# The last expert of a mixture-of-experts layer: scatters made independent, its side work in a new order, part of the output summed by transfers

## Chip, core and metric

The kernel runs on one core of one Trainium2 chip. The metric is the device time of one execution in microseconds (us). A core has five engines that run their own instruction streams: TensorE (PE, matrix products), VectorE (DVE), ScalarE (ACT), GpSimd (POOL) and SyncE (SP, which only issues transfers here). They meet through semaphores. Transfers (DMAs) are issued by SP or by POOL; the indirect ones, with a list of row numbers, come from POOL.

## What is computed

Four layers follow each other, each normalized and added to a running `x` of 4096 tokens by 256 numbers (float32). The change lies in the last one, an expert layer:

```python
    def _L1_ffn_ref(x, Wg, W1, b1, W2, b2):
        ...
        S = jax.nn.sigmoid(xt @ Wg).T
        G, I = jax.lax.top_k(S, k)                 
        ex = xt[I]
        hid = jax.nn.gelu(jnp.einsum('ekh,ehf->ekf', ex, W1) + b1[:, None, :], approximate=False)
        out = (jnp.einsum('ekf,efh->ekh', hid, W2) + b2[:, None, :]) * G[..., None]
        new_x = jnp.zeros_like(xt).at[I.reshape(-1)].add(out.reshape(-1, h))
        return new_x.reshape(b, l, h)
    ...
    x = x + _layernorm(_L1_ffn_ref(_layernorm(x, axis=-1), L1_ffn_Wg, L1_ffn_W1, L1_ffn_b1, L1_ffn_W2, L1_ffn_b2), axis=-1)
```

Each of 8 experts takes its own 1024 best tokens of the 4096. A token may be taken by several experts or by none; its expert outputs are summed, that sum is normalized over its 256 numbers, and `x` is added.

## The kernel before

Tokens lie in 8 blocks of 512 (`TB`), each block as 128 partitions by `NJ` = 4 rows; the blocks of `x` stay on chip as `xs[t]`. At the end of the attention stage `token_rows` (line 1163 and on) writes each block to DRAM twice: normalized rows to `tok_d` and `x` itself to `x_d`. Both are issued by SP.

The expert stage makes, for each expert, a list of its 1024 tokens (`List`), fetches their normalized rows by `List.fetch` (line 1497, eight indirect DMAs of 128 rows from POOL, into `got`), and works in two units of 512 tokens: `feed_forward(u)` with `u` from 0 to 15, expert `e = u // 2`, half `q = u % 2`. A unit has

- eight steps "f" (line 1669): products `ph` of 128 hidden features by 512 tokens, three PSUM buffers, each emptied by ACT with a Gelu into `hid` (line 1676);
- four steps "i" (line 1692): products `py` of 128 tokens by 256 numbers, two PSUM buffers, each emptied by DVE. PE also turns the rows of the next unit (line 1651) after two of them.

For experts 0 to 6, DVE adds the bias and multiplies by the gate into `y` (lines 1706, 1707), and POOL adds `y` to rows of a DRAM tensor `acc_d` by an indirect, accumulating DMA (line 1708). The framework sees each such scatter as a write to the whole of `acc_d`, so each one waits until the one before has landed.

Expert 7 does not scatter its sums. When its turn comes, `with_last_acc` reads `acc_d` back, block by block into `y = ys[t]` (`read_back`, line 1535, on SP; six buffers, of which four lie in the weights of expert 6), and also gathers the rows of expert 7's own tokens: into `accg` from `acc_d`, and into `xg` from `x_d`. Then all 4096 tokens are finished as though there were no expert 7:

- `all_stats(t)`: means and variances on DVE (lines 1526 to 1542), a power and a product on POOL (1530, 1543);
- `all_scaled(t, half)`: four normalizations per block on ACT (1549), in place;
- `all_out(t)`: DVE adds the block to `xs[t]` (1554), SP stores it to the output (1555), and the next block is read back into the freed buffer.

Meanwhile expert 7's tokens are finished on their own: `chosen_known` adds the gated bias to `accg` (1562), the product is added when it leaves PSUM (1718), and `chosen_out` normalizes, adds `xg` and overwrites the tokens' output rows by an indirect DMA (1574 to 1579), which must come after all stores of blocks.

In this stage PE, DVE and ACT run in the order in which the program lists them; POOL and SP are ordered by the framework's scheduler. `asides` is a table of what is listed after each step of expert 7's two units; `aside(u, kind, i)` runs it. In the table before, statistics of block t, its scalings and its sum are spread over steps (0, "f", 6) to (1, "f", 3); the biases of chunks 0 to 3 follow at (0, "f", 7) and (0, "i", 0), and the first four chunks leave at (1, "f", 5).

Of the kernel before, what the change touches and what calls it, by code (L numbers as in the profile page):

```python
# [9 lines left out]
F32 = mybir.dt.float32  # L10
# [8 lines left out]
P = 128  # L19
# [26 lines left out]
CAP = 2  # L46
NSEG = P // NE
NROUND = 15


def bucket_runs():
# [19 lines left out]
def kernel(  # L71
# [961 lines left out]
    with ExitStack() as st3:  # L1033
# [84 lines left out]
        def close(t, h, oT):  # L1118
# [43 lines left out]
                return scale_of("g", xs[t][:, i, :])  # L1162

            def token_rows(i, mean, rs):
                if i == 0:
                    gating["h"] = wk.tile([P, NJ, D], F32, tag="hg", name="hg")
                hg = gating["h"][:, i, :]
                nc.vector.tensor_scalar(hg, xs[t][:, i, :], mean, rs, ALU.subtract, ALU.mult)
                nc.sync.dma_start(tok_d[t * TB + i * P : t * TB + (i + 1) * P, 0:D], hg)
                if i == NJ - 1:  # L1170
                    nc.sync.dma_start(x_d[t * TB : (t + 1) * TB, :].rearrange("(j p) d -> p j d", p=P), xs[t])
                if i % 2:
                    beside.append(lambda: turn_gating(i - 1))
                if i == NJ - 1:
                    beside.append(gate)
# [133 lines left out]
    with ExitStack() as st4:  # L1309
# [132 lines left out]
        class List:  # L1442
# [53 lines left out]

            def fetch(self, dst, rows, c):

                nc.gpsimd.indirect_dma_start(  # L1499
                    out=dst,  # L1500
                    out_offset=None,
                    in_=rows[:, :],
                    in_offset=self.at_chunk(c),
                    bounds_check=NT - 1,
                    oob_is_err=True,
                )
# [2 lines left out]

        out_rows = out.flatten_outer_dims()
        accg = keep.tile([P, NC, D], F32, name="accg")
        xg = keep.tile([P, NC, D], F32, name="xg")
        few = st4.enter_context(tc.tile_pool(name="last", bufs=4))
        stores, ys, room_back = [], {}, []

        def stats_of(tag, tiles):

# [12 lines left out]

        def read_back(t):
            y = room_back[t % len(room_back)]
            nc.sync.dma_start(y, acc_d[t * TB : (t + 1) * TB, :].rearrange("(j p) d -> p j d", p=P))
            ys[t] = [y]

        def all_stats(t):
            y = ys[t][0]
            mv, rs = stats_of("c", [y[:, i, :] for i in range(NJ)])  # L1540
            ms = few.tile([P, NJ], F32, tag="msc", name="msc")
            nc.vector.tensor_scalar(ms, mv[:, :, 0], -1.0, None, ALU.mult)
            nc.gpsimd.tensor_tensor(ms, ms, rs, ALU.mult)
            ys[t] += [rs, ms]

        def all_scaled(t, half):
            y, rs, ms = ys[t]
            for i in (2 * half, 2 * half + 1):
                nc.scalar.activation(  # L1549
                    y[:, i, :], y[:, i, :], AF.Identity, bias=ms[:, i : i + 1], scale=rs[:, i : i + 1]  # L1550
                )

        def all_out(t):
            nc.vector.tensor_tensor(xs[t], xs[t], ys[t][0], ALU.add)  # L1554
            stores.append(nc.sync.dma_start(out_flat[t], xs[t]))
            if t + len(room_back) < NB:
                read_back(t + len(room_back))

        def chosen_known(ks):

            for k in ks:
                nc.vector.scalar_tensor_tensor(
                    accg[:, k, :],
                    mb2[:, NE - 1, :],
                    lists[NE - 1].got[k][:, D + NE - 1 : D + NE],
                    accg[:, k, :],
                    ALU.mult,
                    ALU.add,
                )

        def chosen_out(ks):
            mv, rs = stats_of("d", [accg[:, k, :] for k in ks])
            for i, k in enumerate(ks):
                nc.vector.tensor_scalar(accg[:, k, :], accg[:, k, :], mv[:, i, 0:1], None, ALU.subtract)
            for i, k in enumerate(ks):
                nc.vector.scalar_tensor_tensor(
                    xg[:, k, :], accg[:, k, :], rs[:, i : i + 1], xg[:, k, :], ALU.mult, ALU.add
                )
                scatter = nc.gpsimd.indirect_dma_start(
                    out=out_rows,  # L1580
                    out_offset=lists[NE - 1].at_chunk(k),
                    in_=xg[:, k, :],
                    in_offset=None,
                    bounds_check=NT - 1,
                    oob_is_err=True,
                )
                for store in stores:
                    tc.add_manual_dep(scatter.ins, store.ins.name, over, reason="in the place of")
                for other in replaced:
                    tc.declare_no_dep(scatter.ins, other.ins, reason="an expert's tokens are distinct")  # L1590
                replaced.append(scatter)

        over = mybir.DependencyInfo(mybir.DependencyClass.Sync, mybir.DependencyReason.DATA)
        replaced = []

        def with_last_rows():
            for c in range(NC):
                lists[NE - 1].fetch(xg[:, c, :], x_d, c)

        def with_last_acc():  # L1600

            for tag in ("w1", "w2"):
                free = we.tile([P, 2, NJ, D], F32, tag=tag, name=f"back_{tag}")
                room_back.extend(free[:, k] for k in range(2))
            room_back.extend(wk.tile([P, NJ, D], F32, tag="back", name="back") for _ in range(2))
            for t in range(len(room_back)):
                read_back(t)
            for c in range(NC):
                lists[NE - 1].fetch(accg[:, c, :], acc_d, c)

        def asides():
            at = {}

            def put(where, *steps):
                at.setdefault(where, []).extend(steps)

            places = [(0, "f", 6), (0, "f", 7), *((0, "i", i) for i in range(NJ)), (1, "f", 0), (1, "f", 1)]
            later = [(0, "f", 7), *((0, "i", i) for i in range(NJ)), (1, "f", 0), (1, "f", 1), (1, "f", 2)]  # L1620
            latest = [*((0, "i", i) for i in range(NJ)), (1, "f", 0), (1, "f", 1), (1, "f", 2), (1, "f", 3)]
            for t in range(NB):
                put(later[t], lambda t=t: all_scaled(t, 0))
                put(latest[t], lambda t=t: all_scaled(t, 1), lambda t=t: all_out(t))
                put(places[t], lambda t=t: all_stats(t))
            put((0, "f", 7), lambda: chosen_known((0, 1)))
            put((0, "i", 0), lambda: chosen_known((2, 3)))
            put((1, "f", 4), lambda: chosen_known((4, 5)))
            put((1, "f", 5), lambda: chosen_known((6, 7)), lambda: chosen_out((0, 1, 2, 3)))
            return at  # L1630

        beside_last = asides()

        def aside(u, kind, i):
            e, q = divmod(u, QPE)
            if e == NE - 1:
                for step in beside_last.get((q, kind, i), ()):
                    step()

        QPE = NC // NJ  # L1640
        xT = {}
# [13 lines left out]
        def feed_forward(u):  # L1655
# [32 lines left out]
            for i in range(NJ):  # L1688
# [12 lines left out]
                if i in (1, 2) and u + 1 < NE * QPE:  # L1701
                    turn(u + 1, i - 1)
                gates = lists[e].got[k][:, D + e : D + e + 1]
                if e < NE - 1:
                    y = wk.tile([P, D], F32, tag="y", name="y", bufs=4)
                    nc.vector.tensor_tensor(y, py, mb2[:, e, :], ALU.add)  # L1706
                    nc.vector.tensor_scalar(y, y, gates, None, ALU.mult)
                    nc.gpsimd.indirect_dma_start(  # L1708
                        out=acc_d[:, :],
                        out_offset=lists[e].at_chunk(k),  # L1710
                        in_=y,
                        in_offset=None,
                        bounds_check=NT - 1,
                        oob_is_err=True,
                        compute_op=ALU.add,
                    )
                else:
                    nc.vector.scalar_tensor_tensor(accg[:, k, :], py, gates, accg[:, k, :], ALU.mult, ALU.add)  # L1718
                    aside(u, "i", i)
                    if q:  # L1720
                        chosen_out((k,))

        lists[0].chunks()
        for part in range(4):
# [1 line left out]
            lists[0].collect(part)  # L1726
        lists[0].gather()
        for u in range(NE * QPE):
            if u == (NE - 1) * QPE:
                with_last_acc()  # L1730
            feed_forward(u)
            e, q = divmod(u, QPE)
            if u == (NE - 1) * QPE - 2:
                with_last_rows()
            if q == QPE - 1 and e + 2 < NE:
                weights.append(load_expert(e + 2))

# [33 lines left out]
```

## Time and profile before

| what | us |
|---|---|
| median of 3 runs (1650.67 to 1650.97) | 1650.72 |
| the profiled execution, own time | 1650.91 |
| its span, first to last instruction | 1648.8 |
| PE busy | 1550.9 (94%) |
| DVE busy | 926.6 (56%) |
| ACT busy | 634.3 (38%) |
| POOL busy | 399.7 (24%) |
| expert 7 begins on PE (unit 14) | 1565.45 |
| last product of expert 7 ends | 1639.64 |

A profile's line of a timeline has: start, length, engine, line of the kernel, operation, output<-inputs, shape, how many were merged, and in brackets how long that engine sat idle before it and what released it. "PEld" are weight loads, which run beside the products. Idle time of an engine counts only where another one then waits for it. The DMA share is the mean busy share of the core's 16 DMA engines.

### The profile page before, as it was taken

The page shows a single profiled execution, that of the slowest core. Times are in us where ns is not written, and L with a number is a line of the kernel's source. Part 1 is how long each engine was busy: PE and PEld are TensorE (multiplying, and loading weights), DVE is VectorE, ACT ScalarE, POOL GpSimd, SP SyncE. Part 2 cuts the span into 40 slices and gives each one's busy share as a digit, 9 for nine tenths or more (in the row PEclk, how much of TensorE's full clock was granted, in tenths as well). Part 3 has the DMA queues.
Part 4 walks back from the last instruction along what each step waited for, and adds up shares of the span by engine and source line. Part 5 has one row for each costly group of instructions (what it writes and reads, how often), then busy time and mean ns, then how long its engine had stood idle before and what let it go on. Part 6 is the DMA issues. An engine that isn't in the chain of part 4 may idle for free. (4 is left out here: it accounts for less than half of the span.)

```text
span 1648.8 us, 22341 instructions
## 1 busy us (share of the span) xinstructions
PE 1550.9 (94%) x8663; PEld 770.9 (47%) x8663; DVE 926.6 (56%) x2090; ACT 634.3 (38%) x1101; POOL 399.7 (24%) x434
## 2 busy tenths in 40 slices
PE   7999999999999999999999999922999999999986
PEld 3666666665222232323232222211766675766754
DVE  4555566663667787878787888776222122121245
ACT  3344444434554545454545454520211212112133
POOL 4123232322201020202011111012333332332643
PEclk9999999999999999999999999965999999999998
DMA  8300000000000000000000000050134233323362
GB/s 211 111 1 1 1 1 1 1 1 1 1 1 1 14 14 14 14 14 14 1 26 1 27 14 14 20 162 24 39 78 90 65 66 79 68 65 74 68 179 87
DMA packets 71028, 68.51 MB, mean 42 GB/s; under 512 B 23277, under 2 KB 65162, under 8 KB 70794
## 3 DMA queue, kind: packets, MB, share of 16 engines
q1 hardware_dynamic: 57760, 47.01, 9.4%
q0 software_dynamic: 12288, 19.15, 6.3%
q8 instruction: 68, 1.11, 0.3%
q10 hardware_dynamic: 874, 0.93, 0.2%
q14 instruction: 38, 0.31, 0.1%
HBM read 41.74 MB, written 25.33 MB: 41 GB/s over the span
## 5 line engine op out<-in xcount | busy, mean ns | idle before, releaser
L1233 DVE TENSOR_SCALAR w<-sc 128x1024 f32<-128x1024 f32 x256 | 312.7, 1222 | 97.4 <-PE sc L1223 65.1
L1232 ACT ACTIVATE w<-sc 128x512 f32<-128x512 f32 x512 | 278.0, 594 | 229.6 <-PE sc L1223 102.5
L1223 PE MATMUL sc<-qT,kT 32*128 32x512 f32 x2048 | 293.6, 639 | 1.4 <-ACT w L1232 0.8
L1239 PE MATMUL po<-w,vaug 128*17 128x512 f32 x2048 | 274.7, 598 | 1.3 <-DVE turned L1271 0.3
L1692 PE MATMUL py<-w,hid 128*128 128x256 f32 x1024 | 232.9, 384 | 6.9 <-DVE accg L1718 6.9
L1669 PE MATMUL ph<-xT,w 128*128 128x512 f32 (+1 forms) x544 | 228.5, 578 | 4.7 <-ACT hid L1676 4.2
L1676 ACT ACTIVATE hid<-ph,mb 128x512 f32<-128x512 f32 (+1 forms) x136 | 89.9, 661 | 345.6 <-PE ph L1669 342.7
L1692 PEld LDWEIGHTS py<-w,hid 128*128 128x128 f32 x1024 | 192.9, 192 | 40.2 <-DVE accg L1718 7.4
L1223 PEld LDWEIGHTS sc<-qT,kT 32*128 32x128 f32 x2048 | 80.8, 183 | 184.8 <-issue 170.7
L1669 PEld LDWEIGHTS ph<-xT,w 128*128 128x128 f32 x544 | 105.4, 195 | 118.8 <-issue 107.4
L1239 PEld LDWEIGHTS po<-w,vaug 128*17 128x17 f32 x2048 | 35.3, 95 | 200.3 <-issue 171.0
L1708 POOL DMA_INDIRECT acc_d<-y,idx x56 | 88.5, 1580 | 166.5 <-issue 139.5
L1706 DVE TENSOR_TENSOR y<-py,mb 128x256 f32<-128x256 f32 x56 | 23.4, 418 | 142.8 <-PE py L1692 135.5
L1499 POOL DMA_INDIRECT got<-tok_d,idx x64 | 65.8, 1028 | 151.6 <-DVE idx L1489 134.5
L1653 DVE COPY xT<-tp 128x512 f32<-128x512 f32 (+1 forms) x34 | 22.3, 660 | 90.9 <-PE tp L1651 90.9
L1059 POOL TENSOR_TENSOR rsg<-veg,mhalf 128x1 f32<-128x1 f32 x32 | 17.7, 553 | 219.5 <-DVE veg L1058 219.5
L683 PE MATMUL pg<-nT,wh 128*128 128x512 f32 x128 | 61.5, 613 | 1.5 <-ACT nT L622 1.5
L791 PE MATMUL py<-wo,oT 128*128 128x256 f32 x256 | 61.9, 385 | 0.0
L699 PE MATMUL pv<-wh,nT 128*128 128x512 f32 x128 | 59.7, 592 | 0.0
L1489 DVE CAST idx<-parts 128x8 int32<-128x8 f32 x8 | 1.3, 167 | 101.8 <-PE parts L1487 101.8
L791 PEld LDWEIGHTS py<-wo,oT 128*128 128x128 f32 x256 | 47.3, 190 | 17.2 <-issue 9.4
L564 POOL TENSOR_TENSOR x<-x,y 128x1024 f32<-128x1024 f32 x14 | 32.9, 2351 | 73.3 <-ACT y L553 73.3
(273 smaller groups left out, 1889.2 us busy)
## 6 DMA issues: line engine op xcount, KB each, us to landing
w<-in_L_ffn_W_dram SPq DMA_DIRECT2D x16, 1024.0 KB, 5.7
x<-in_L_attn_x_dram SPq DMA_DIRECT2D x8, 512.0 KB, 7.6
acc_d<-logits SPq DMA_DIRECT2D x8, 512.0 KB, 4.6
x_d<-x SPq DMA_DIRECT2D x8, 512.0 KB, 3.0
tok_d<-hg SPq DMA_DIRECT2D x32, 128.0 KB, 1.7
out_dram<-x SPq DMA_DIRECT2D x8, 512.0 KB, 2.9
back_w<-acc_d SPq DMA_DIRECT2D x6, 512.0 KB, 5.4
wh<-in_L_attn_Wh_dram SPq DMA_DIRECT2D x2, 512.0 KB
```

The source lines that it names most:

```text
L683: nc.tensor.matmul(pg, lhsT=wh[:, c, HID + e * P : HID + (e + 1) * P], rhs=d["nT"][:, c, :], start=(c == 0), stop=(c == DC - 1),)
L699: nc.tensor.matmul(pv, lhsT=d["nT"][:, c, i * P : (i + 1) * P], rhs=wh[:, c, 0:HID], start=(c == 0), stop=(c == DC - 1),)
L791: nc.tensor.matmul(py, lhsT=d["oT"][:, e, :], rhs=wo[:, e, :], start=(e == 0), stop=(e == EC - 1))
L1223: nc.tensor.matmul(sc, lhsT=row["kT"][t][rows, r, kt * P : (kt + 1) * P], rhs=row["qT"][rows, t, qh * TB : (qh + 1) * TB], start=True, sto ...
L1232: nc.scalar.activation(w[:, j, :], sc, AF.Relu)
L1233: nc.vector.tensor_scalar(w[:, 2:4, :], pair, 0.0, None, ALU.max)
L1239: nc.tensor.matmul(po[32 * j : 32 * j + HD + 1, :], lhsT=row["v"][:, kt, HQ * t + 2 * j + r, :], rhs=w[:, j, :], start=(kt == 0), stop=(kt ...
L1499: nc.gpsimd.indirect_dma_start(out=dst, out_offset=None, in_=rows[:, :], in_offset=self.at_chunk(c), bounds_check=NT - 1, oob_is_err=True,)
L1669: nc.tensor.matmul(ph, lhsT=w1[:, c, f * P : (f + 1) * P], rhs=xT[u][:, c, h * n : (h + 1) * n], start=(c == 0), stop=(c == DC - 1),)
L1676: nc.scalar.activation(hid[:, f, h * n : (h + 1) * n], ph, AF.Gelu, bias=mb1[:, e * FC + f : e * FC + f + 1])
L1692: nc.tensor.matmul(py, lhsT=hid[:, f, i * P : (i + 1) * P], rhs=w2[:, f, :], start=(f == 0), stop=(f == FC - 1),)
L1708: nc.gpsimd.indirect_dma_start(out=acc_d[:, :], out_offset=lists[e].at_chunk(k), in_=y, in_offset=None, bounds_check=NT - 1, oob_is_err=Tr ...
```

## The change

Four things are changed.

1. In `token_rows`, the first `ADDED` = 5 blocks of `x` are also stored to the output tensor, in four pieces each, during the attention stage.
2. For those blocks `all_out` does not add on DVE: POOL issues a DMA that adds the normalized block to the output rows in DRAM. The read-back of these blocks puts four neighbouring tokens into one partition, so that its rows and those of the accumulating store are 4 KB long. Blocks 5 to 7 go as before.
3. The eight scatters of expert 6 are declared independent of each other, the first still waiting for expert 5's last. What reads `acc_d` afterwards (the read-backs and the gathers into `accg`) is made to wait for all eight. `xg` is now fetched between expert 6's two units, and `accg` in three parts, four, two and two chunks.
4. The table of side work is written out anew, and POOL too runs in listed order from expert 6 on.

```diff
+ADDED = 5
...
             def token_rows(i, mean, rs):
+                if t < ADDED:
+                    nc.sync.dma_start(out_flat[t][:, i, :], xs[t][:, i, :])
...
+        out_tokens = out.flatten_outer_dims()
+        out_rows = out_tokens.rearrange("(t p j) d -> t p j d", p=P, j=NJ)
...
+        def after_all(one, others):
+            for other in others:
+                tc.add_manual_dep(one.ins, other.ins.name, all_rows, reason="all rows")
+
+        def beside_each_other(one, others):
+            for other in others:
+                tc.declare_no_dep(one.ins, other.ins, reason="an expert's tokens are distinct")
+            others.append(one)
...
-            nc.sync.dma_start(y, acc_d[t * TB : (t + 1) * TB, :].rearrange("(j p) d -> p j d", p=P))
+            rows = "(p j) d -> p j d" if t < ADDED else "(j p) d -> p j d"
+            after_all(nc.sync.dma_start(y, acc_d[t * TB : (t + 1) * TB, :].rearrange(rows, p=P)), summed)
...
         def all_out(t):
-            nc.vector.tensor_tensor(xs[t], xs[t], ys[t][0], ALU.add)
-            stores.append(nc.sync.dma_start(out_flat[t], xs[t]))
+            y = ys[t][0]
+            if t < ADDED:
+                stores.append(nc.gpsimd.dma_start(out_rows[t], y, accum_op=ALU.add))
+            else:
+                nc.vector.tensor_tensor(xs[t], xs[t], y, ALU.add)
+                stores.append(nc.sync.dma_start(out_flat[t], xs[t]))
             if t + len(room_back) < NB:
                 read_back(t + len(room_back))
...
+        def fetch_acc(*cs):
+            for c in cs:
+                after_all(last.fetch(accg[:, c, :], acc_d, c), summed)
...
+        def chosen_out(*ks):
+            for k in ks:
                 scatter = nc.gpsimd.indirect_dma_start(
-                    out=out_rows,
-                    out_offset=lists[NE - 1].at_chunk(k),
+                    out=out_tokens,
+                    out_offset=last.at_chunk(k),
...
+                after_all(scatter, stores)
+                beside_each_other(scatter, replaced)
...
+        front, back = (0, 1), (2, 3)
+        beside_last = {
+            (0, "f", 5): [(all_stats, 0)],
+            (0, "f", 6): [(all_stats, 1)],
+            (0, "f", 7): [(all_scaled, 0), (known, 0), (all_stats, 2), (fetch_acc, 4, 5)],
+            (0, "i", 0): [(all_out, 0), (all_scaled, 1), (known, 1), (all_stats, 3)],
+            (0, "i", 1): [(all_out, 1), (all_scaled, 2), (known, 2), (all_stats, 4), (fetch_acc, 6, 7)],
+            (0, "i", 2): [(all_out, 2), (all_scaled, 3), (known, 3)],
+            (0, "i", 3): [(all_out, 3), (all_scaled, 4), (all_stats, 5)],
+            (1, "f", 0): [(all_out, 4)],
+            (1, "f", 1): [(all_scaled, 5, front), (all_stats, 6)],
+            (1, "f", 2): [(all_scaled, 5, back), (all_stats, 7)],
+            (1, "f", 3): [(all_scaled, 6, front), (all_out, 5)],
+            (1, "f", 4): [(all_scaled, 6, back), (chosen_stats, 0, 1, 2, 3)],
+            (1, "f", 5): [(all_scaled, 7, front), (all_out, 6)],
+            (1, "f", 6): [(all_scaled, 7, back), (chosen_less_mean, 0, 1, 2, 3)],
+            (1, "f", 7): [(all_out, 7), (known, 4, 5, 6, 7)],
+            (1, "i", 0): [(chosen_sum, 0, 1, 2, 3), (chosen_stats, 4), (chosen_less_mean, 4), (chosen_out, 0, 1, 2, 3)],
+            (1, "i", 1): [(chosen_sum, 4), (chosen_stats, 5), (chosen_less_mean, 5), (chosen_out, 4)],
+            (1, "i", 2): [
+                (chosen_sum, 5), (chosen_out, 5), (chosen_stats, 6), (chosen_less_mean, 6), (chosen_sum, 6), (chosen_out, 6)
+            ],
+            (1, "i", 3): [(chosen_stats, 7), (chosen_less_mean, 7), (chosen_sum, 7), (chosen_out, 7)],
+        }
...
+                if e == NE - 1:
                     nc.vector.scalar_tensor_tensor(accg[:, k, :], py, gates, accg[:, k, :], ALU.mult, ALU.add)
                     aside(u, "i", i)
-                    if q:
-                        chosen_out((k,))
+                    continue
...
+                if e == NE - 2:
+
+                    beside_each_other(scatter, summed)
...
         for u in range(NE * QPE):
-            if u == (NE - 1) * QPE:
-                with_last_acc()
+            e, q = divmod(u, QPE)
+            if u == (NE - 2) * QPE:
+                st4.enter_context(tc.manual_schedule(engines={engines.Pool}))
+            elif u == (NE - 1) * QPE - 1:
+                for c in range(NC):
+                    last.fetch(xg[:, c, :], x_d, c)
+            elif u == (NE - 1) * QPE:
+                begin_last()
             feed_forward(u)
-            e, q = divmod(u, QPE)
-            if u == (NE - 1) * QPE - 2:
-                with_last_rows()
```

The arithmetic of the old helper functions is kept: `known` is `chosen_known`, and `chosen_stats`, `chosen_less_mean`, `chosen_sum` and the new `chosen_out` are the four parts of the old `chosen_out`. `begin_last` is `with_last_acc` with only the first four gathers into `accg`.

## The prediction

> **What bounds the kernel now.** I read the page first (busy slices), then stretches of the last expert, then the timelines of TensorE (PE), VectorE (DVE) and GpSimd (POOL) there, then the DMA view. Times are us from the span's start. Page, busy tenths:
>
> ```profile
> PE   7999999999999999999999999922999999999986
> PEclk9999999999999999999999999965999999999998
> ```
>
> PE is full except in the routing stage (slices 27, 28), which the change does not touch, and at the end. Only the end is at stake. The stretches below are a whole unit of 512 tokens of expert 6; then the last expert: first products of its unit 14, second products of 14, first of 15, second of 15, the tail. Columns: sum, PE, PEld, DVE, ACT, POOL busy, PE clock, DMA share, GB/s.
>
> ```profile
> 1537.02:1565.45 28.43, 28.43 (x106) 19.02 (x104) 4.31 (x10) 5.50 (x8) 16.32 (x14) 1.00 0.37 65
> 1565.45:1579.18 13.73, 13.73 (x33) 6.08 (x32) 0.85 (x2) 4.81 (x7) 4.74 (x4) 1.00 0.25 30
> 1579.18:1603.92 24.74, 17.79 (x73) 14.81 (x72) 16.00 (x56) 7.77 (x15) 14.01 (x16) 0.86 0.79 256
> 1603.92:1625.65 21.73, 17.55 (x33) 6.94 (x32) 16.13 (x58) 13.31 (x26) 6.84 (x9) 0.84 0.42 144
> 1625.65:1639.64 13.99, 13.98 (x65) 11.97 (x63) 8.65 (x26) 0.69 (x1) 9.39 (x11) 1.00 0.16 57
> 1639.64:1648.80 9.16, 0.00 (x0) 0.00 (x0) 1.99 (x6) 0.00 (x0) 2.09 (x3) 0.74 0.08 30
> ```
>
> An undisturbed unit is 28.43, its first half 13.73, so the second half is 14.70. Third row: 24.74 - 14.70 = 10.0 lost. Fourth: 21.73 - 13.73 = 8.0 lost. So PE loses 18.0, and a tail of 9.2 follows. Where, in PE's timeline:
>
> ```profile
> 1588.44 3.72 PE L1692 MATMUL py<-w,hid 128*128 128x256 f32 x16 [1.76 <-DVE accg L1718]
> ...
> 1597.79 6.29 PE L1692 MATMUL py<-w,hid 128*128 128x256 f32 x16 [5.19 <-DVE accg L1718]
> ...
> 1617.35 8.46 PE L1669 MATMUL ph<-xT,w 128*128 128x512 f32 x12 [3.63 <-ACT hid L1676]
> ```
>
> PE waits for DVE to free one of two `py` buffers, then for ACT to free a `ph`. DVE and POOL say why:
>
> ```profile
> 1566.11 0.42 DVE L1707 TENSOR_SCALAR y<-y,got 128x256 f32<-128x256 f32 x1
> 1582.18 1.41 DVE L1526 BATCH_NORM_STATS2 stc<-back_w 128x6 f32<-128x256 f32 x4 [15.65 <-DMA back_w<-acc_d]
> ...
> 1587.51 0.48 DVE L1562 SCALAR_TENSOR_TENSOR accg<-mb,got,accg 128x256 f32<-128x256 f32 x1 [1.12 <-DMA accg<-acc_d,idx]
> ```
>
> ```profile
> 1569.95 1.55 POOL L1708 DMA_INDIRECT acc_d<-y,idx  x1 [3.02 <-issue]
> 1574.44 1.56 POOL L1708 DMA_INDIRECT acc_d<-y,idx  x1 [2.94 <-issue]
> 1579.03 1.08 POOL L1499 DMA_INDIRECT accg<-acc_d,idx  x1 [3.03 <-DMA acc_d<-y,idx]
> ...
> 1642.55 1.05 POOL L1579 DMA_INDIRECT out_dram<-xg,idx  x1 [0.81 <-DVE xg L1576]
> ```
>
> The last `y` of expert 6 is ready at 1566.5, but its scatter starts at 1574.44, because each waits for the landing of the one before (pitch 4.6 against 1.56 of issue). It lands at 1578.24 (3.8 after its start); only then are the sums read back, and DVE has idled 15.65. Late, DVE has statistics and five whole-block adds between PE's evictions. What a scatter-add costs the DMA engines, 1556 to 1578:
>
> ```profile
> q0 software_dynamic: 720, 0.66, 26.5%
> ```
>
> That is 26.5% x 22 / 5 = 1.17 for each 128 KB. Slices inside reach 130 to 180 GB/s; the read-backs run near 350.
>
> **What the Trainium skill says.** "DMA: Bandwidth & Descriptors", Rules for kernel authors: an accumulate reads its destination and writes it later, so one must wait for an earlier one on the same bytes. That is the 4.6 pitch; distinct tokens do not need it. Same page, "Issuing engines are not separate DMA queues": SP's and POOL's transfers share 16 engines. The trace agrees: the second gather of `accg`, issued at 1580.4 among read-backs, holds DVE until 1587.51. "TensorE: Matmul & The Clock Gate", Part 1: an idle window of about 3.4 us halves the clock. The trace agrees: after 5.19 idle, 16 matmuls take 6.29 instead of 3.62, and after 3.63 the next are slow too. So the stalls cost more than their length.
>
> **Part by part.**
>
> *Early stores.* 20 stores of 128 KB on SP in the attention stage: 20 x 0.37 = 7.5 of issue in 340 us, where SP works some 20 per block and DMA shares are near 0. Behind them on SP wait `x_d` and `tok_d` rows needed after 1100; the last three blocks have no such stores. So 0. Uncovered it would be 1.5 per block.
>
> *Independent scatters, `xg` fetched between units.* Scatters 0 to 3: 1537.04 + 4 x 1.87 (1.56 + 0.31 gap) = 1544.6; eight `xg` gathers of 1.32 to 1555.2, just when the next `y` (1555.2) is ready; from there `y` comes every 3.9, so the last scatter issues at 1566.6 and lands at 1570.4: 7.8 sooner.
>
> *Unit 14.* Read-backs issue at 1570.4; the first lands 3.8 to 5 later, the others each 1.5 apart (0.52 MB at 350 GB/s), the sixth by 1583.5. DVE: statistics of 1.87 (1.31 + 0.29 + 0.18 + 0.07) for blocks 0, 1, one bias of 0.4, block 2: done about 1581.5. PE's first second product ends at 1579.18 + 3.46 = 1582.6, so DVE is free for it: the 1.76 goes. To 1593.9 DVE has 4 x 0.45 + 3 x 0.4 + 2 x 0.6 + 2 x 1.87 = 7.9 in 11.2: the 5.19 goes, with the slow clock. Unit 15 starts at 1593.9, not 1603.9.
>
> *POOL.* New: five accumulating stores. No plain DMA from POOL is in the trace; nearest rows are 1.01 (gather) and 1.56 (scatter-add) for 128 rows. I take 1.5, from 1.0 to 6.2 (if 4 KB rows cost as four 1 KB rows). A power with its product is 1.2 to 2.2; I take 1.4. From 1581.5: power 1582.9, two gathers 1585.5, store 0 1587.0, power 1588.4, store 1 1589.9, power (statistics 1590.6) 1592.0, two gathers 1594.7, stores 2 and 3 1597.7, power of block 5 1599.1, store 4 1600.6.
>
> *ACT in unit 15.* Gelu 0.57 and two scalings 1.08 = 1.65 per step of 1.72. The first scaling of block 5 could start at 1598.1, the power comes at 1599.1: 1.0 late, never recovered. PE: 1.0.
>
> *Transfers.* 512 KB accumulated: 4 x 1.17 = 4.7 at the measured mean, which includes each ramp; 2.9 to 4.0 at 130 to 180 GB/s; I take 3.1, range 2.4 to 4.7 (2.4 since wider rows may go faster). Read-back 6 reuses block 0's buffer and waits for store 0: 1587.0 + 3.1 + 2 = 1592, landed 1597; read-back 7: 1595, landed 1600. Statistics of 7 at 1602, power 1603.5, scaling due at 1605.4. It fits by 2.
>
> *Tail.* PE's fifth product ends at 1611.1 + 1.0 = 1612.1; eviction 0.45, four sums 1.67, statistics 0.78, power 0.6: scatter 0 at 1615.7. It waits for all stores: 5 x 3.1 + 2 x 1.5 + 0.8 + 3 x 1.5 = 23.8 of transfers from 1587.0 is 1611; the last store, issued about 1610, lands 2.9 later. Not late. But POOL now has four scatters queued there, which before went at 1627.4, ahead of the last products: 4 x 1.29, power 0.58, two scatters 2.58, power and sum 1.1, scatter 1.29, power and sum 1.2: scatter 7 at 1627.6, which is 5.0 after PE's end (1622.6), where before it is 2.9. Cost 2.1.
>
> **Sum.** -18.0 + 1.0 + 2.1 = -14.9. From the last scatter to the end stays 6.25: 1633.9. The execution's own time is 2.1 above its span, and the median shown 0.2 below that: 1635.8, say 1636.
>
> **Rivals.**
> 1. *Stores transfer slowly* (4.7 each). For: the measured mean. Against: it contains each ramp. Transfers end 8 later, about 1619 to 1620, so scatter 0 waits 4; read-back 7 lands 2 to 3 late, which ACT then passes to PE in part. 4 to 8 lost: about 1642.
> 2. *The start does not move* (scatters still follow one another or the reads do not start sooner). For: POOL also waits on landings of older DMAs. Against: the gathers at a pitch of 1.32 show several in flight. 7.8 later, of which the lighter DVE recovers little: about 1644.
> 3. *Slower: POOL's issue of the accumulating stores.* If one takes 6.2, POOL, in order, delays the powers behind; ACT waits for them with Gelus queued behind, and PE for ACT. All five lie in one chain up to the power of block 6, so each us costs 5, less 2 of slack: 1636 + 5 x 4.7 - 2 = 1657. Break-even near 5 (14.9 + 2 = 5 x 3.4). Against: the scatter-add's 1.56 is for 128 rows, and this store has 128 rows too.
>
> **Chances.** Forecast 0.62; rival 1 0.22; rival 2 0.06; rival 3 and other losses of that size 0.08; a plain zero 0.02. All but the last two are faster. Floor: no ACT or tail cost, 1632.7. Range 1632 to 1645 takes in the forecast and rivals 1 and 2. Faster 0.90, within 0.2% (3.3 us, about what a measurement here can tell) 0.02, slower 0.08.
>
> **What would show it.** First statistics of `back_w` near 1575; no PE gap over 1 between 1579 and 1594 and its clock at 1.00; store issues of 1 to 2 on POOL; scatter 0 near 1616 waiting for DVE's sums rather than a store; the last scatter about 5 after PE's end. Wrong: a store issue over 3 us on POOL, PE waiting for Gelu behind a scaling, or scatter 0 waiting for a landing.

## The result, and the profile after

The kernel after takes 1637.07 us, median of 4 runs (1636.75 to 1637.47); the kernel before, on the same chip, 1650.70 (4 runs). The ratio is 0.9916, 95% interval 0.9904 to 0.9929. The forecast was 1636, range 1632 to 1645. The profiled execution's own time is 1637.27 and its span 1635.4, 13.4 below the span before.

The page of the kernel after, busy tenths:

```profile
PE   7999999999999999999999999941999999999996
PEclk9999999999999999999999999965899999999998
```

The row of PE ended in 86 and had 22 in the routing stage; now it ends in 96, and the slices lie a little differently over a shorter span, which turns 22 into 41. At this grain only the end has changed. The stretches of expert 7 after, cut at the same events as before (first products of unit 14, second of 14, first of 15, second of 15, tail); columns as before: sum, PE, PEld, DVE, ACT, POOL busy, PE clock, DMA share, GB/s.

```profile
1566.44:1580.17 13.73, 13.73 (x33) 6.08 (x32) 5.67 (x26) 4.81 (x7) 8.15 (x9) 1.00 0.71 213
1580.17:1594.87 14.70, 14.70 (x74) 12.94 (x72) 8.71 (x37) 10.73 (x21) 9.37 (x12) 1.00 0.80 196
1594.87:1608.60 13.73, 13.73 (x33) 6.08 (x32) 11.35 (x46) 10.53 (x19) 8.79 (x11) 1.00 0.98 233
1608.60:1622.58 13.98, 13.98 (x65) 11.97 (x63) 8.69 (x23) 0.84 (x2) 5.77 (x7) 1.00 0.26 92
1622.58:1635.40 12.82, 0.00 (x0) 0.00 (x0) 3.35 (x12) 0.00 (x0) 5.14 (x6) 0.59 0.11 41
```

In every stretch but the tail, PE's busy time is the whole stretch and its clock is 1.00. 24.74 has become 14.70 and 21.73 has become 13.73, so all 18.0 are back. The tail has grown from 9.16 to 12.82. From the start of unit 14 to the end of the span: 83.35 before, 68.96 after, so -14.4 = -18.0 + 3.66. The spans differ by only 13.4 because unit 14 starts 1.0 later (1566.44 against 1565.45), which is taken up below. PE's timeline after has no bracket left; before it had four in these stretches, of 1.76, 5.19, 0.56 and 3.63:

```profile
1580.18 7.07 PE L1713 MATMUL py<-w,hid 128*128 128x256 f32 x32
...
1594.87 13.90 PE L1690 MATMUL ph<-xT,w 128*128 128x512 f32 x32
1608.60 13.98 PE L1713 MATMUL py<-w,hid 128*128 128x256 f32 x64
```

DVE and ACT after: the last gated `y` of expert 6 and the first statistics of a block read back; then a Gelu and the scalings of blocks 5 to 7 in unit 15.

```profile
1567.10 0.35 DVE L1731 TENSOR_SCALAR y<-y,got 128x256 f32<-128x256 f32 x1
1574.87 1.41 DVE L1543 BATCH_NORM_STATS2 stc<-back_w 128x6 f32<-128x256 f32 x4 [7.41 <-DMA back_w<-acc_d]
```

```profile
1598.50 0.69 ACT L1697 ACTIVATE hid<-ph,mb 128x512 f32<-128x512 f32 x1 [0.97 <-PE ph L1690]
1599.09 1.08 ACT L1567 ACTIVATE back<-back,msc,rsc 128x256 f32<-128x256 f32 x2
```

DVE's idle time before its first statistics has gone from 15.65 to 7.41. ACT's first scaling of block 5 has no bracket: its power did not keep it waiting. POOL after: the last scatter of expert 6, the first gather of `accg`, two accumulating stores with a power between them, and the tail.

```profile
1567.73 1.55 POOL L1732 DMA_INDIRECT acc_d<-y,idx  x1 [1.30 <-DVE y L1731]
1572.29 1.09 POOL L1502 DMA_INDIRECT accg<-acc_d,idx  x1 [3.01 <-DMA acc_d<-y,idx]
...
1585.60 1.06 POOL L1574 DMA_DIRECT2D out_dram<-back_w  x1
...
1597.51 1.09 POOL L1547 TENSOR_TENSOR rsc<-vec,mhalf 128x4 f32<-128x4 f32 x1
1598.68 0.20 POOL L1561 TENSOR_TENSOR msc<-msc,rsc 128x4 f32<-128x4 f32 x1
1599.19 0.91 POOL L1574 DMA_DIRECT2D out_dram<-back  x1 [0.31 <-ACT hid L1697]
...
1615.14 0.59 POOL L1547 TENSOR_TENSOR rsd<-ved,mhalf 128x1 f32<-128x1 f32 x1 [9.12 <-DVE ved L1546]
1616.29 1.32 POOL L1606 DMA_INDIRECT out_dram<-xg,idx  x1 [0.56 <-issue]
...
1628.70 1.05 POOL L1606 DMA_INDIRECT out_dram<-xg,idx  x1 [0.81 <-DVE xg L1602]
```

The last scatter-add is released by DVE's `y` and no longer by the landing of the one before. A store costs POOL 0.91 to 1.06. The last scatter to the output starts 6.1 after PE's last product (1622.58); before it was 2.9. The DMA engines from 1595 to 1605, while three of the adding stores are in flight (packets' MB and share of the 16 engines):

```profile
q0 software_dynamic: 463, 1.64, 84.1%
```

84.1% of 10 us is 8.41 for 1.64 MB. Over the time that was theirs this is about 195 GB/s, or 2.7 per 512 KB; it is an estimate, since this queue also carries the end of two gathers of `accg`.

### The profile page after: what moved, and what is told of

The parts are those of the page before. It is cut to its first block, busy times and chain, and to the rows that moved or that the text cites. A ratio compares the mean times of both kernels' runs of the same rounds, so it can differ in the third digit from the quotient of the medians.

```text
span 1635.4 us, 22372 instructions
## 1 busy us (share of the span) xinstructions
PE 1544.9 (94%) x8663; PEld 769.3 (47%) x8663; DVE 920.3 (56%) x2085; ACT 634.4 (39%) x1101; POOL 403.1 (25%) x439
## 4 chain that ended last, share of the span: by engine, by line
PE 90%; issue 4%; DVE 3%; POOL 1%; ACT 1%; DMA 1%; SPq 0%; POOLq 0%; ACTq 0%; DVEq 0%
PE sc L1226 16%; PE po L1242 16%; PE ph L1690 13%; PE py L1713 13%; PE py L792 4%; PE pg L684 3%; PE pv L700 3%; PE pt L1128 2%; PE ph L848 2%; PE po L764 2%; PE pv L373 2%; PE pq L349 2%; PE pq L869 2%; PE po L768 2%; PE pk L349 2%
## 5 line engine op out<-in xcount | busy, mean ns | idle before, releaser
L1690 PE MATMUL ph<-xT,w 128*128 128x512 f32 (+1 forms) x544 | 225.0, 572 | 0.5 <-DVE xT L1674 0.4
```

The source lines that it names most:

```text
L1690: nc.tensor.matmul(ph, lhsT=w1[:, c, f * P : (f + 1) * P], rhs=xT[u][:, c, h * n : (h + 1) * n], start=(c == 0), stop=(c == DC - 1),)
```

## The experiments

All ratios are to the kernel before, run on the same chip in the same session. The pitch of a row of instructions is the time from one start to the next; a transfer has landed when all of it has arrived.

**Which part brings the time.** Four kernels. The first adds to the kernel before only the independence of expert 6's scatters (and the waits of the readers on all eight); order, table and stores stay as they were:

```diff
 # the kernel before
+            after_all(nc.sync.dma_start(y, acc_d[...]), summed)
...
+                    if e == NE - 2:
+                        for other in summed:
+                            tc.declare_no_dep(scatter.ins, other.ins, reason="an expert's tokens are distinct")
+                        summed.append(scatter)
```

> The kernel before, with one part of the change alone: the scatters of expert 6 are independent of each other (and the readers of their sums wait for all eight). Table of side work, sums on DVE and their stores as before. Theory (most of the gain is the earlier start, since DVE and ACT have nearly enough time in PE's shadow once they start 7 us sooner): DVE needs some 4.05 per second-product step of unit 14 where PE takes 3.9, ACT 2.6 in three of eight steps of unit 15 where PE takes 1.7 with three buffers, so PE loses 2 to 4 instead of 18, and the tail keeps its 2.9 from PE's end to the last scatter: 1634 to 1637, that is about the changed kernel's 1637 or a little less. Rival (the new table and the accumulating stores are what lets DVE and ACT keep up): PE still loses 8 or more, 1641 to 1645.

Measured: 1643.66, ratio 0.9958 (0.9941 to 0.9975), in the rival's range: about half of the gain. Its stretch of the second products of unit 14 is 14.69, as after: independence alone brings back those 10.0. Its last scatter starts at 1567.89, so the framework's own order of POOL did not lose the gain either. But the first products of unit 15 take longer than before:

```profile
1595.02:1618.71 23.69, 16.49 (x33) 6.29 (x32) 18.01 (x60) 14.49 (x27) 8.48 (x10) 0.93 0.47 154
```

23.69 - 13.73 = 10.0 lost, where before it was 8.0: the earlier start gains 10.0 and the next wait takes 2.0 of it. PE there waits for a Gelu at a pitch of 4.0 where 1.72 would do:

```profile
1605.49 1.98 PE L1675 MATMUL ph<-xT,w 128*128 128x512 f32 x4 [2.01 <-ACT hid L1682]
1609.49 1.98 PE L1675 MATMUL ph<-xT,w 128*128 128x512 f32 x4 [2.01 <-ACT hid L1682]
```

DVE, POOL and ACT of the same kernel show who holds the Gelu:

```profile
1602.46 1.22 DVE L1560 TENSOR_TENSOR x<-x,back 128x1024 f32<-128x1024 f32 x1 [0.83 <-ACT back L1555]
1603.60 1.40 DVE L1532 BATCH_NORM_STATS2 stc<-back_w 128x6 f32<-128x256 f32 x4
...
1610.45 1.23 DVE L1560 TENSOR_TENSOR x<-x,back_w 128x1024 f32<-128x1024 f32 x1 [0.83 <-ACT back_w L1555]
```

```profile
1605.70 1.01 POOL L1536 TENSOR_TENSOR rsc<-vec,mhalf 128x4 f32<-128x4 f32 x1 [1.96 <-DVE msc L1548]
1606.78 0.95 POOL L1549 TENSOR_TENSOR msc<-msc,rsc 128x4 f32<-128x4 f32 x1
```

```profile
1607.77 1.09 ACT L1555 ACTIVATE back_w<-back_w,msc,rsc 128x256 f32<-128x256 f32 x2 [1.35 <-POOL msc L1549]
1608.77 0.67 ACT L1682 ACTIVATE hid<-ph,mb 128x512 f32<-128x512 f32 x1
```

Read from the top: DVE adds block t, only then takes the statistics of block t+2, which is listed behind it (1603.60); POOL makes the power and product (1605.70 to 1607.73); ACT waits for them, scales, does one Gelu, scales again; DVE waits for that to add block t+2 (1610.45). That is a loop of 8.0 for two blocks, 4.0 for each, through three engines, none of which is full. PE is a bystander whose Gelu stands between two scalings. DVE of the kernel before shows the same loop, 8.15 from the sum of block 4 to that of block 6, around PE's wait of 3.63:

```profile
1610.17 1.23 DVE L1554 TENSOR_TENSOR x<-x,back 128x1024 f32<-128x1024 f32 x1 [1.92 <-ACT back L1549]
1611.31 1.40 DVE L1526 BATCH_NORM_STATS2 stc<-back_w 128x6 f32<-128x256 f32 x4
...
1618.32 1.23 DVE L1554 TENSOR_TENSOR x<-x,back_w 128x1024 f32<-128x1024 f32 x1 [1.91 <-ACT back_w L1549]
```

The second kernel is the one after with expert 6's scatters chained again:

```diff
 # the kernel after
-                if e == NE - 2:
-
-                    beside_each_other(scatter, summed)
```

> The changed kernel with the scatters of expert 6 chained again; all else as changed. Theory of the prediction taken literally (independence brings the start 7.8 forward): 1643 to 1645. Theory from the trace of the changed kernel: with the xg gathers moved between the units, scatter 4 goes when its y is ready, and a chain at a pitch of 4.55 against y's 3.9, 3.9 and 2.9 makes the last scatter only 2.4 later (1570.1 against 1567.7); DVE has 2.4 of idle time ahead of its first eviction, so 1637 to 1639.

Measured: 1647.35, 0.9977 (0.9967 to 0.9987), slower than either number. POOL's timeline says why. (It is that of the slowest of nine executions, 1651.33, where the others took 1645.66 to 1648.49, so its waits are probably longer than the usual ones.)

```profile
1553.28 1.56 POOL L1732 DMA_INDIRECT acc_d<-y,idx  x1 [3.02 <-issue]
...
1564.51 1.11 POOL L1502 DMA_INDIRECT xg<-x_d,idx  x1 [0.30 <-issue]
1565.93 1.62 POOL L1732 DMA_INDIRECT acc_d<-y,idx  x1 [0.30 <-issue]
...
1580.41 1.55 POOL L1732 DMA_INDIRECT acc_d<-y,idx  x1 [4.00 <-issue]
```

With POOL in listed order, the eight gathers of `xg` stand behind four chained scatters (pitch 4.6), and the next four scatters, chained too, behind the gathers. Counted from the start of unit 14, the last starts 12.5 later than after, not the 7.7 by which it is late before. PE then waits 6.86 in unit 14, and 2.55 and 0.86 in the second products of unit 15. So the listed order of the fourth change, with the gathers of `xg` where the third puts them, needs the independent scatters: without them the last scatter starts 5 later than in the kernel before.

The same trace shows something else. The start is late here, and yet the first products of unit 15 take 13.73 (1603.57 to 1617.30) without a wait:

```profile
1603.57 13.90 PE L1690 MATMUL ph<-xT,w 128*128 128x512 f32 x32
```

PE's 2.55 and 0.86 follow right behind it, and there ACT and DVE wait for the read-back of block 7 (DVE for 5.73), a late landing and not the loop. So the new table with POOL in listed order avoids the loop without the earlier start too.

The third and fourth separate the adding stores: `ADDED = 0` in the kernel after (all eight blocks summed on DVE and stored by SP, the rest as after), and the early stores alone in the kernel before (20 stores more, the output unchanged since the later stores overwrite them).

```diff
 # the third, the kernel after
-ADDED = 5
+ADDED = 0
```

```diff
 # the fourth, the kernel before
+                if t < ADDED:
+                    nc.sync.dma_start(out_flat[t][:, i, :], xs[t][:, i, :])
```

> The changed kernel with ADDED = 0: all eight blocks are added to x on DVE and stored by SP, read back in the old layout, no early stores. Theory (DVE had room in the new table): five adds of 1.13 more, one of them 0.5 late for PE and the power of block 5 about 0.8 late for ACT; 1637 to 1639.5. Rival (taking the adds off DVE carries the gain): DVE again late for PE's two buffers, 1641 or more.

> The kernel before with only the early stores of five blocks of x added (they are overwritten later by the same stores as before). Theory (hidden): 1650 to 1651.5, as before. Rival (they cost the 1.0 by which the last expert starts later in the changed kernel's trace): 1651.5 to 1652.

Measured: 1636.84, 0.9915 (0.9898 to 0.9931), for the third; 1650.33, 0.9997 (0.9988 to 1.0006), for the fourth. The early stores cost nothing, as predicted. And the sums added by transfers bring nothing: without them PE is just as free of gaps. DVE then has five adds of 1.2 more in units 14 and 15, and room for them: in that trace it stands idle for ACT ahead of only the last of its eight adds (0.80), so hardly any statistics are held up behind an add. Of the four changes, then, the third and the fourth carry the gain, and the first two bring nothing here.

**Whether the loop is the order of the statistics.** The first kernel again, with the statistics of block t+2 listed ahead of the sum of block t:

```diff
 # the first kernel
             for t in range(NB):
+                put(places[t], lambda t=t: all_stats(t))
+            for t in range(NB):
                 put(later[t], lambda t=t: all_scaled(t, 0))
                 put(latest[t], lambda t=t: all_scaled(t, 1), lambda t=t: all_out(t))
-                put(places[t], lambda t=t: all_stats(t))
```

> The kernel with independent scatters alone (1643.7), and in each step of the old table of side work the statistics of block t+2 listed ahead of the sum of block t instead of behind it. Nothing else. Theory (unit 15 there loses 10 to a ring: sum of block t on DVE, then statistics of t+2 behind it, power on POOL, scalings on ACT with a Gelu between, then the sum of t+2; 8.0 for two blocks, 3.99 a step where PE needs 1.72): with the statistics ahead the ring is broken, ACT's surplus in four steps (2.6 for 1.72) costs 1 to 3 of the 10, and the tail stays at 2.9: 1634.5 to 1637. Rival (DVE or ACT is simply full there): 1641 to 1644.

Measured: 1639.66, 0.9930 (0.9915 to 0.9945), between the two. The loss in the first products of unit 15 falls from 10.0 to 4.65 (1595.32 to 1613.70): the order of the statistics is over half of it, and not the whole. A possible reason for a part of the remainder is on POOL:

```profile
1605.29 1.92 POOL L1536 TENSOR_TENSOR rsc<-vec,mhalf 128x4 f32<-128x4 f32 x1 [0.87 <-DVE msc L1548]
1607.29 1.12 POOL L1549 TENSOR_TENSOR msc<-msc,rsc 128x4 f32<-128x4 f32 x1
```

The power takes 1.92 where the first kernel's takes 1.01, because it now runs beside DVE's add (1605.13 to 1606.35), and the product 1.12 where 0.20 is usual, beside the next add (from 1607.13). The Trainium skill says so ("GPSIMD Engine Reference", Specifications): GpSimd's access to SBUF is shared with VectorE, and they contend when a DVE instruction has two inputs in SBUF. The add has two, the statistics one; the traces agree, with 0.9 for each of the two. That this holds PE up is not shown, however: in the trace of the third kernel two powers take 1.96 and 2.05, ACT waits 1.79 behind the first of them, and PE loses nothing. Which of the other changes (halves of blocks in turn, biases moved, POOL in listed order, `accg` in three parts) recovers the other 4.65 was not separated.

**Whether POOL's issue is the danger.** Rival 3 priced a long issue on POOL. Here two small DMAs (one number for each of 128 rows, into scratch that no output uses) stand ahead of each adding store:

```diff
 # the kernel after
             if t < ADDED:
+                for n in range(EXTRA):
+                    nc.gpsimd.dma_start(spare_d[t, n], ys[t][1][:, 0:1])
                 stores.append(nc.gpsimd.dma_start(out_rows[t], y, accum_op=ALU.add))
```

> The changed kernel with two small transfers (one number of each of 128 rows, to scratch memory) issued by POOL ahead of each of the five accumulating stores, to price POOL's time in that place. Theory (rival 3 of the prediction, with sizes from the trace of the changed kernel: an issue takes 0.95, so each store's place grows by 1.9): the power of block 5 comes 5.5 late for ACT and that of block 6 some 0.8 more, ACT cannot catch up: 1641 to 1644. By the prediction's own formula (5 for each us, less 2 of slack, from 1.5): 1641. Rival (POOL's place does not matter, because DVE's or the transfers' time binds): 1637 to 1638.5.

Measured: 1661.26, 1.0052 (1.0037 to 1.0068), far above both. The time of the extra issues is not enough for that: two take 1.18, so all ten take 5.9. POOL and DVE of that kernel, in the slowest of its four executions (1666.09; the fastest took 1656.87):

```profile
1597.88 1.17 POOL L1577 DMA_DIRECT2D spare_d<-rsc  x2
1603.14 0.91 POOL L1578 DMA_DIRECT2D out_dram<-back_w  x1 [4.09 <-issue]
```

```profile
1613.71 1.41 DVE L1545 BATCH_NORM_STATS2 stc<-back_w 128x6 f32<-128x256 f32 x4 [17.12 <-DMA back_w<-acc_d]
```

POOL stands for 4.09 ahead of a store with no releaser that the profile shows; at two other places in this trace it waits for the landing of `spare_d` by name (3.10 and 1.89). And the read-back of block 6, which needs the buffer of an adding store, holds DVE for 17.12. PE loses 6.50, 4.29 and 11.59 behind Gelus. Three things are seen to be late in this trace, and none of them is POOL's time for an issue.

- The landing of the first adding store. SP waits 28.8 for it before it can read block 6 back; in the kernel after, 16.6.
- The transfers beside the small ones. From 1588 to 1593 POOL's queue moves only 0.21 MB, some 43 GB/s, none of it in packets under 512 bytes, although the time of its packets adds up to 127% of what the 16 engines have. The adding stores of the kernel after had about 195 GB/s.
- The power of block 4, which waits 3.10 for the landing of a small transfer, because that transfer reads the tile that the power is to write. The experiment itself made this wait.

So this kernel prices late landings and not POOL's issue; a longer issue alone was not tried. The Trainium skill ("DMA: Bandwidth & Descriptors", Rules for kernel authors) calls transfers under 64 KB mostly overhead. Ten of 0.5 KB cost about 24 us here (20 to 29 in single executions), but that is not overhead of their own: what the trace shows is that larger transfers beside them became slow, and why they did stays open.

**What holds the tail.** Two kernels move the first four scatters ahead of the statistics of chunk 4 in the table, so that the power of chunk 4 no longer stands ahead of them on POOL: one is the kernel after, the other has `ADDED = 0` as well.

```diff
-            (1, "i", 0): [(chosen_sum, 0, 1, 2, 3), (chosen_stats, 4), (chosen_less_mean, 4), (chosen_out, 0, 1, 2, 3)],
+            (1, "i", 0): [(chosen_sum, 0, 1, 2, 3), (chosen_out, 0, 1, 2, 3), (chosen_stats, 4), (chosen_less_mean, 4)],
```

> The changed kernel with one entry reordered: after the fifth product the first four scatters of expert 7 are listed ahead of the statistics of chunk 4, not behind them. Theory (the tail is POOL's chain from scatter 0 on, 12.4 long, and scatter 0 there waits for a power that it does not need): scatter 0 starts near 1613, when its sum is ready and the last store has landed, not at 1616.3; the last scatter 2.4 to 2.8 sooner, within 3.5 of PE's end: 1634 to 1635. Rival (the last scatter waits for PE's last product whatever POOL does): 1636.8 to 1637.3.

> As the run before, and ADDED = 0: all sums on DVE, no accumulating and no early stores. Theory (the accumulating stores are worth nothing): the same within 0.7 as the run with accumulating stores, 1633.5 to 1635.5; the last of eight stores lands about 0.6 later, which may delay scatter 0 by as much. Rival (stores on SP gate scatter 0): 1636 to 1637.

Measured: 1636.82, 0.9914 (0.9900 to 0.9928), and 1638.06, 0.9920 (0.9906 to 0.9934). No gain. The two medians lie 1.2 apart (their ranges overlap), not within 0.7. The first of the two on POOL:

```profile
1615.18 1.15 POOL L1606 DMA_INDIRECT out_dram<-xg,idx  x1 [8.80 <-DVE std L1543]
...
1620.22 0.58 POOL L1547 TENSOR_TENSOR rsd<-ved,mhalf 128x1 f32<-128x1 f32 x1
```

Scatter 0 starts 1.1 sooner, but now the power of chunk 4 stands behind four scatters, DVE waits 4.30 for it, and every later chunk follows: the last scatter is 6.5 after PE's end. Turning the order round moves the time from one side of POOL's queue to the other. That points at the powers themselves. The last kernel is the one after with those of chunks 4 to 7 taken off POOL: the root on ACT, which is idle by then, a reciprocal on DVE, and a root of one column behind the last scaling so that ACT's table is loaded before it is needed.

```diff
 # the kernel after, stats_of; the tag "e" is that of chunks 4 to 7
-            nc.gpsimd.tensor_tensor(rs[:, :n], ve[:, :n], mhalf[:, :n], ALU.pow)
+            if tag == "e":
+                nc.scalar.activation(rs[:, :n], ve[:, :n], AF.Sqrt)
+            else:
+                nc.gpsimd.tensor_tensor(rs[:, :n], ve[:, :n], mhalf[:, :n], ALU.pow)
...
+        def root_ready():
+            none = few.tile([P, 1], F32, tag="none", name="none")
+            nc.scalar.activation(none, ys[NB - 1][0][:, NJ - 1, 0:1], AF.Sqrt, scale=0.0)
+
+        def chosen_late(*ks):
+            for k in ks:
+                mv, rs = stats_of("e", [accg[:, k, :]])
+                chosen[k] = mv[:, 0, 0:1], rs[:, 0:1]
+                chosen_less_mean(k)
+                nc.vector.reciprocal(rs[:, 0:1], rs[:, 0:1])
+                chosen_sum(k)
...
+            (1, "f", 7): [(all_out, 7), (known, 4, 5, 6, 7), (root_ready,)],
+            (1, "i", 0): [(chosen_sum, 0, 1, 2, 3), (chosen_late, 4), (chosen_out, 0, 1, 2, 3, 4)],
+            (1, "i", 1): [(chosen_late, 5), (chosen_out, 5)],
+            (1, "i", 2): [(chosen_late, 6), (chosen_out, 6)],
+            (1, "i", 3): [(chosen_late, 7), (chosen_out, 7)],
```

> The kernel after, with the roots of the last four chunks (4 to 7) moved from POOL to ACT, which has nothing to do after its last scaling (its table for the root is loaded ahead by a root of one column, behind the last scaling), with a reciprocal on DVE, so that POOL issues nothing but the eight scatters in the tail, and each chunk's sum follows its statistics at once. The output is the same but for the rounding of the roots. Theory: the tail is held by POOL, which needs 12.4 us from scatter 0 (1616.3) to the start of scatter 7 (1628.7): 7 x 1.32 of scatters, 3 x 0.58 of powers, 1.4 of gaps between the two. Without the powers scatter 0 starts at about 1615.3 and the chain of DVE after PE's end decides: scatter 7 about 2.9 to 3.5 after PE's end instead of 6.1, 1633.5 to 1634.5 us. Rival: POOL's pace of scatters comes from the landings of its earlier transfers and not from what it issues, or scatter 0 still waits for the last store: 1636 to 1637.

Measured: 1633.22 (1632.47 to 1633.63), 0.9889 (0.9873 to 0.9906), the fastest of all; its four runs lie below all four of the kernel after. POOL and ACT:

```profile
1614.68 1.15 POOL L1621 DMA_INDIRECT out_dram<-xg,idx  x1 [9.27 <-DVE vee L1546]
...
1624.58 0.97 POOL L1621 DMA_INDIRECT out_dram<-xg,idx  x1 [1.00 <-issue]
```

```profile
1608.89 1.28 ACT L1601 ACT_TABLE_LOAD   x1
...
1614.48 0.20 ACT L1548 ACTIVATE rse<-vee 128x1 f32<-128x1 f32 x1 [4.09 <-DVE vee L1546]
```

From scatter 0 to scatter 7 it takes 9.9 instead of 12.4, and the last scatter starts 2.6 after PE's end (1607.98 + 13.98 = 1621.96) instead of 6.1. Of the 4.1 by which its span is shorter (1631.3), 3.5 are that, and 0.6 an earlier start of the last products, which is no part of the edit. The edit also lists each chunk's sum right behind its statistics, and this was not separated from the move of the powers. But in the kernel after, DVE's sums of chunks 5 to 7 stand 2.46, 1.81 and 0.50 waiting for POOL's powers, and in this trace no sum waits for POOL. The load of ACT's table, 1.28, is hidden. The Trainium skill ("ScalarE activation tables: per-element evaluation and per-set limits", What a function is on this engine) gives 1283 ns for it; the trace agrees.

What holds scatter 0, once no power stands ahead of it, is likely the landing of the last block's store. In the last two traces shown it starts 1.7 and 2.2 after the first of DVE's sums is ready (1613.5 and 1612.5), and in the DMA view of the last kernel the bytes of the last store move until about 1613.5. The two kernels with the scatters first come near to a trial: DVE begins the first of the sums at 1613.01 in one and at 1612.99 without adding stores, but the add ahead of the last store ends at 1610.36 and 1611.10, and scatter 0 starts at 1615.18 and 1615.96. It moves with the store (0.74 and 0.78) and not with its sum. It was not tried by itself.

## Why the prediction was right, point by point

- *PE's 18.0.* Right, to 0.0. But the grounds given for the second half of it were incomplete. The prediction let the earlier start and the smaller load on DVE recover unit 15's 8.0. The first and third kernels show that the earlier start alone makes it 10.0, and that DVE's five adds don't matter. The 8.0 come from the new table (with POOL in listed order), which breaks a loop over three engines that the prediction did not name: it read PE's wait for a `ph`, and DVE's fullness, and did not follow the wait on through ACT and POOL back to DVE. Its sum for the new table, ACT's 1.65 in each step of 1.72, did hold. That the old loss would come back whole followed from that sum and not from the account of the loss, so this part was right with some luck.
- *Sums 7.8 sooner.* Right: the first reader of the sums on POOL starts 5.85 after unit 14 begins (1572.29 - 1566.44), before it was 13.58 (1579.03 - 1565.45), so 7.7. The reason was right too: independence alone moves it as far.
- *Unit 14.* Right: both stalls and the slow clock are gone with the earlier start alone. First statistics were said to come near 1575 and come at 1574.87.
- *The slow clock.* The idle window of about 3.4 that the prediction cites fits the 5.19 and the 3.63 of the kernel before. It is no lower bound in these traces, though: in the kernel with the early stores alone an idle time of 1.98 is followed by a granted clock of 0.50 to 0.54 (1589.5 to 1592.5), and 16 products take 5.41 instead of 3.62. After 1.76 in the kernel before, the clock stayed at 1.00. The forecast does not hang on it, since the kernel after has no gap.

```profile
1589.54 5.41 PE L1695 MATMUL py<-w,hid 128*128 128x256 f32 x16 [1.98 <-DVE accg L1721]
```

- *Early stores.* Right: nothing.
- *POOL's store issue, 1.5 within 1.0 to 6.2.* Too high: 0.91 to 1.06, so even the lower bound was slightly too high, and the 6.2 of rival 3 did not come. The nearest row was the gather (1.01) and not the scatter-add (1.55).
- *ACT in unit 15, +1.0.* It was 0: with the shorter issues the product of block 5 is done at 1598.88, and ACT goes from its Gelu to the scaling at 1599.09 without a pause.
- *Store transfer, 3.1 per 512 KB.* 2.7, inside the range. The product of block 7 comes at 1603.2; its scaling is due at 1605.95, so 2.7 to spare where 2 was said.
- *Tail, last scatter 5.0 after PE's end.* The mis-sized term: 6.1. Scatter 0 is 0.6 later than said, and the way to scatter 7 takes 12.4 instead of 11.9, because POOL waits 0.81 for DVE's sum between a power and each of the last two scatters (brackets above): power and sum take 1.38 and 1.37 where 1.1 and 1.2 were said. From the last scatter to the end it is 6.7, not 6.25; why is open. Together the tail costs 3.66 and not 2.1.
- *The sum.* Said -14.9, found -14.4 from the start of unit 14. That it comes so near is partly luck: ACT's 1.0 didn't come, and the tail cost 1.6 more than said. PE ends at 1622.58 where 1622.6 was said, also by two errors that cancel: ACT's 1.0 didn't come, and unit 14 began 1.0 later. That start isn't due to the early stores: the first kernel of the experiments, without them, begins unit 14 at 1566.60, and the one with the small DMAs, which has them, at 1565.50. In the traces of the eleven kernels the start lies between 1565.45 and 1566.89; the cause of that spread stays open.

Rival 1 was wrong in its size (4.7 against 2.7), and rival 2 in its premise. With the scatters chained again, its kernel takes 1647 against the 1644 that were said.

## What to carry to other kernels

When a wait of PE ends on ACT or DVE, follow it on until it comes back to where it began: a loop over several engines costs its whole length at each turn although none of them is full, and the order of two listed steps can shorten it (here the loss fell from 10.0 to 4.65). When an engine with an ordered queue mixes long issues with short steps of a chain (here scatters and powers), turning the order round may only move the wait, as it did here; the short steps can go to an engine that is idle there. An edit that makes one part fast may be needed by another (the listed order by the independent scatters), so undo each part alone before crediting it.

## What the runs showed that was not expected

- POOL needs less for a direct accumulating store of 128 rows of 4 KB (0.91 to 1.06) than for an indirect scatter-add of 128 rows of 1 KB (1.55).
- Accumulating stores moved about 195 GB/s, counted over the share of the DMA engines' time that they took; the read-backs ran near 350.
- Ten transfers of 0.5 KB, issued in about 0.6 each, made the kernel about 24 us slower: larger transfers beside them landed late.
- An idle time of 1.98 on PE was followed by half the granted clock.
- POOL's power goes from 1.01 to 1.92, and its product from 0.20 to about 1, beside DVE's adds of two inputs.
